# Splitting five of the seven block products of proj once more, for the last two batches of a cross-attention block

## The chip, the core and the metric

The kernel runs on one core of one Trainium2 chip, as one program. The time is device microseconds of that core. TensorE (PE) does the matrix products into PSUM, VectorE (DVE), ScalarE (ACT) and GpSimd (POOL) work on elements, and SyncE (SP) issues most DMAs. [...] Each engine takes its instructions strictly in the order of the program and waits at an instruction until what it needs is there.

## The reference, cut to what matters

```
for each of 4 batches (512 query rows, 512 context rows, D = 512, all float32):
    q, k, v  = layer_norm(x) @ q_w + q_b,  enc @ k_w + k_b,  enc @ v_w + v_b     # 16 heads of 32
    hidden   = softmax(q k^T / sqrt(32), masked) v @ cproj_w + cproj_b + x
    y        = layer_norm(hidden) @ fc_w + fc_b          # 512 x 512 times 512 x 2048
    y        = gelu_tanh(y) @ proj_w + proj_b            # 512 x 2048 times 2048 x 512
    out      = hidden + y
```

The change concerns the last product, proj, of batches two and three (the batches are counted from zero).

## The kernel before, in words

**Stages.** Up to about 550 us the attention of all four batches runs, with the MLP (fc, GELU, proj) of batch zero and half of that of batch one woven into it by lists written out by hand (`first`, `later`). What remains is written out in `last_mlps` (L590): for batch one its second half, then for batches two and three the whole MLP, each as fc, then proj. Within it the order of the program is the order of work on every engine; there is no planner.

**fc.** The 2048 columns of fc are worked off in eight pairs of 128. `fc_seven` (L483) makes a pair as a 2 x 2 block product with seven products in place of eight (Strassen's method in Winograd's form): it needs four sums of the weights and four of the input, and joins the seven products with a few additions. The input's sums are made once per batch by `y_sums` (L472), the sums of the pair's weights by `sum_wa` (L580), one pair ahead. Both run on VectorE. The pair's weights are loaded two pairs ahead by SP into `wa`, their sums lie in `ws`; both are parts of the tile `gt`. TensorE makes the products in the order q1, q26, q57, q34; the second half of q26 (s2 t2) is the first that needs sums. VectorE joins them (L501, L505, L506, L509) into `ga`, and ScalarE applies GELU in place.

**proj.** `project` (L613) does the same for the second product: the activations `ga` are split into four blocks g11, g12, g21, g22, each 128 x 8 chunks x 256, the weights `pb` into b11 to b22. `g_sums` makes the activation sums s1, s2, s4 in `gs` and s3 in place of g21, two chunks at a time under fc. `p_sums` (L584) makes the weight sums t1, t2, t4 in `pt` and t3 in place of b12. Seven products follow: q1, q2, q3, q6, q7, q5, q4. Each is made by `product` (L619) at L622: two row tiles, eight chunks, a matmul with 128 x 128 stationary and 256 moving columns, so 16 matmuls of the program. In float32 the profile records two matmuls for each. VectorE and GpSimd join the products into the residual rows `hid` (`join`, L629); VectorE takes those that lie in PSUM, GpSimd those that were copied to SBUF (`p1p`, `u2p`, `u3p`). SP stores the rows.

**What lies between.** Inside proj the callbacks `sums`, `turns` and `middle` prepare the next batch. `sums` calls `p_sums` and loads the next batch's residual rows (`load_hid`, L397), to which GpSimd adds a bias (`add_row`, L357). `turns` transposes the next batch's normalized rows on TensorE (`ln2_turn`), with two of the four results written by VectorE (L162) and two by ScalarE. `middle` makes `y_sums` of the next batch and `sum_wa(0)`.

**Weights of proj.** Batch one's second half of proj needs only chunk pairs 4 to 7 of `pb`, whose sums are made before `last_mlps`. Pairs 0 to 3 share their place with the attention's keys and queries and with the last batch's rows; they are loaded by SP (L679) under batch two's fc and summed in batch two's `sums`. Batch three uses the same weights and sums again.

**PSUM.** Two pools of four banks each, `ps_acc` and `ps_last`; a block product takes one bank.

## Time and profile before

| | us |
|---|---|
| median of three runs | 803.38 (802.66 to 807.0) |
| the profiled execution, its own time | 801.93 |
| its span, first to last instruction | 800.2 |
| granted TensorE clock, mean | 0.998 |
| TensorE busy | 785.3 (98%) |
| VectorE busy | 573.8 (72%) |
| ScalarE busy | 339.5 (42%) |
| GpSimd busy | 123.9 (15%) |

The stages of `last_mlps` on the span's clock, by where the chain of work passes from one to the next:

| stage | us from the span's start |
|---|---|
| batch one: fc, second half | 552 to 576 |
| batch one: proj, second half | 576 to 601.3 |
| batch two: fc | 601.3 to 649.9 |
| batch two: proj | 649.9 to 700.2 |
| batch three: fc | 700.2 to 748.6 |
| batch three: proj | 748.6 to 800.2 |

The lines of a timeline give the start in us, the time, the engine, the source line, the operation, the tiles out<-in by the program's names, the shapes and how many instructions were merged; in brackets stand the idle time in front and what ended it. The table by stage gives for each engine the busy time in a stretch and the number of instructions, then the granted clock, the busy share of the DMA engines and their GB/s.

### The profile page before, as it was taken

The page shows a single profiled execution, that of the slowest core. Times are in us where ns is not written, and L with a number is a line of the kernel's source. Part 1 is how long each engine was busy: PE and PEld are TensorE (multiplying, and loading weights), DVE is VectorE, ACT ScalarE, POOL GpSimd, SP SyncE. Part 2 cuts the span into 40 slices and gives each one's busy share as a digit, 9 for nine tenths or more (in the row PEclk, how much of TensorE's full clock was granted, in tenths as well). Part 3 has the DMA queues.
Part 4 walks back from the last instruction along what each step waited for, and adds up shares of the span by engine and source line. Part 5 has one row for each costly group of instructions (what it writes and reads, how often), then busy time and mean ns, then how long its engine had stood idle before and what let it go on. Part 6 is the DMA issues. An engine that isn't in the chain of part 4 may idle for free.

```text
span 800.2 us, 12085 instructions
## 1 busy us (share of the span) xinstructions
PE 785.3 (98%) x4178; PEld 499.4 (62%) x4178; DVE 573.8 (72%) x1179; ACT 339.5 (42%) x745; POOL 123.9 (15%) x146
## 2 busy tenths in 40 slices
PE   9999999989999999999999999999999999999998
PEld 6545455456655645556553433446888888888887
DVE  3789998888888857779878988546738983368511
ACT  2567765547763636456554479500201220022100
POOL 1210030055121141001220100020040020200011
PEclk9999999999999999999999999999999999999999
DMA  8889999847897777787777799882325330033001
GB/s 325 289 230 241 235 237 244 231 115 182 209 240 196 211 210 192 179 198 199 181 173 213 205 261 246 202 254 93 117 84 172 118 106 14 27 86 86 1 14 40
DMA packets 60957, 137.15 MB, mean 171 GB/s; under 512 B 12464, under 2 KB 15664, under 8 KB 60768
## 3 DMA queue, kind: packets, MB, share of 16 engines
q1 hardware_dynamic: 59472, 132.43, 61.3%
q0 software_dynamic: 896, 2.82, 1.1%
q10 hardware_dynamic: 528, 1.14, 0.7%
q8 instruction: 33, 0.54, 0.3%
q14 instruction: 28, 0.23, 0.1%
HBM read 58.22 MB, written 6.82 MB: 81 GB/s over the span
## 4 chain that ended last, share of the span: by engine, by line
PE 87%; DVE 6%; SPq 3%; ACT 1%; issue 1%; DMA 1%; POOL 0%; DVEq 0%; POOLq 0%; ACTq 0%
PE q L495 20%; PE accp L554 8%; PE sc L262 7%; PE accc L386 7%; PE av L345 7%; PE accv L240 6%; PE acck L218 6%; PE accq L228 5%; PE accf L536 3%; DVE ptt L266 3%; SPq L328 2%; PE q4p L622 2%; PE q3p L622 2%; PE q5p L622 2%; PE q6p L622 2%; PE q7p L622 2%
## 5 line engine op out<-in xcount | busy, mean ns | idle before, releaser
L270 ACT ACTIVATE ptt<-ptt,mn 128x512 f32<-128x512 f32 x256 | 181.7, 711 | 135.1 <-DVE mn L266 134.8
L266 DVE CUSTOM_DVE_ANT_0 ptt<-sc,mb 128x512 f32<-128x512 f32 x256 | 161.0, 685 | 32.7 <-PE sc L262 32.4
L285 DVE STREAM_TRANSPOSE tb<-ptt 128x1024 f32<-128x1024 f32 x96 | 119.2, 1242 | 14.4 <-ACT ptt L270 12.9
L554 PE MATMUL accp<-pbt,gt 128*128 128x512 f32 x192 | 86.7, 600 | 0.0
L495 PE MATMUL q<-yT,gt 128*128 128x256 f32 x320 | 78.9, 379 | 0.0
L262 PE MATMUL sc<-pbt 32*128 32x512 f32 x512 | 73.0, 640 | 4.7 <-DVE mn L266 2.5
L513 ACT ACTIVATE ga<-ga,vec 128x512 f32<-128x512 f32 x40 | 26.7, 714 | 93.2 <-DVE ga L455 93.2
L495 PEld LDWEIGHTS q<-yT,gt 128*128 128x128 f32 x320 | 60.8, 190 | 8.7 <-issue 0.5
L554 PEld LDWEIGHTS accp<-pbt,gt 128*128 128x128 f32 x192 | 35.2, 190 | 49.0 <-issue 46.4
L240 PEld LDWEIGHTS accv<-ptt,xe 128*128 128x128 f32 x512 | 58.7, 192 | 9.5 <-issue 6.7
L495 PE MATMUL q<-ys,gt 128*128 128x256 f32 x240 | 61.8, 380 | 0.5 <-DVE ys L452 0.5
L240 PE MATMUL accv<-ptt,xe 128*128 128x128 f32 x512 | 60.8, 277 | 0.0
L218 PE MATMUL acck<-xe,ptt 128*128 128x512 f32 x128 | 59.1, 605 | 0.0
L228 PE MATMUL accq<-xe,ptt 128*128 128x512 f32 x128 | 58.4, 599 | 0.0
L386 PE MATMUL accc<-wc,oT 128*128 128x512 f32 x128 | 56.6, 596 | 0.0
L495 PEld LDWEIGHTS q<-ys,gt 128*128 128x128 f32 x240 | 45.4, 190 | 7.4 <-DVE ys L452 0.9
L345 PE MATMUL av<-pT,v 128*32 128x256 f32 x768 | 48.1, 392 | 1.8 <-DMA gt<-tb 0.7
L498 ACT COPY p<-q 128x256 f32<-128x256 f32 x28 | 9.9, 355 | 92.5 <-PE q L495 92.5
L270 ACT ACTIVATION_READ_ACCUMULATOR ptt<-ptt,mn 128x1 f32 x256 | 47.8, 187 | 0.0
L252 POOL TENSOR_TENSOR v<-v,row 128x512 f32<-128x512 f32 x16 | 20.4, 1275 | 172.9 <-ACT v L245 172.8
L228 PEld LDWEIGHTS accq<-xe,ptt 128*128 128x128 f32 x128 | 23.6, 190 | 32.4 <-issue 30.4
L262 PEld LDWEIGHTS sc<-pbt 32*128 32x128 f32 x512 | 20.0, 182 | 37.9 <-issue 21.4
(137 smaller groups left out, 1071.4 us busy)
## 6 DMA issues: line engine op xcount, KB each, us to landing
pT<-tb SPq DMA_DIRECT2D x384, 136.0 KB, 2.4
pbt<-p_w_dram SPq DMA_DIRECT2D x40, 256.0 KB, 3.1
gt<-fc_w_dram SPq DMA_DIRECT2D x40, 256.0 KB, 2.6
gt<-tb SPq DMA_DIRECT2D x64, 136.0 KB, 3.4
xe<-tb SPq DMA_DIRECT2D x56, 136.0 KB, 3.1
pbt<-fc_w_dram SPq DMA_DIRECT2D x24, 256.0 KB, 3.9
ptt<-k_w_dram SPq DMA_DIRECT2D x16, 256.0 KB, 3.8
xe<-encT_dram SPq DMA_DIRECT2D x16, 256.0 KB, 4.6
```

The costliest lines, as they stand in the source:

```text
L218: nc.tensor.matmul(acc, S["wk", w][:, d, :], eT[:, d, :], start=(d == 0), stop=(d == ND - 1))
L228: nc.tensor.matmul(acc, S["wq", w][:, d, :], xT[:, d, :], start=(d == 0), stop=(d == ND - 1))
L240: nc.tensor.matmul(acc[:, ts(t, P)], eT[:, d, ts(t, P)], S["wv", w][:, d, :], start=(d == 0), stop=(d == ND - 1),)
L262: nc.tensor.matmul(sc[:, h, :], qT[r, ts(qt, P)], kT[r, :], start=True, stop=True)
L266: nc.vector.tensor_tensor_reduce(out=s, in0=sc[:, h, :], in1=S["mb", w // NG], scale=1.0, scalar=FMAX, op0=ALU.add, op1=ALU.min, accum_out=mn,
L270: nc.scalar.activation(s, s, AF.Exp, bias=mn, scale=-1.0, accum_out=sums[:, qt, h : h + 1])
L285: nc.vector.transpose(*two_heads[k])
L345: nc.tensor.matmul(av[ts(h, HD), : 2 * P].rearrange(shape, **kw), v[:, t, ts(h, HD)], p[t][h], start=(t == 0), stop=(t == NT - 1),)
L386: nc.tensor.matmul(acc, S["oT", b][:, g, ts(t, P)], wc[:, g, :], start=(g == 0), stop=(g == NG - 1))
L495: nc.tensor.matmul(o, x[:, k], y[:, k], start=(k == 0), stop=(k == 1))
L554: nc.tensor.matmul(acc, gT[q % 2][:, k, ts(t, P)], S["pw", b, q * FQ + k], start=(k == 0), stop=(k == FQ - 1))
L622: nc.tensor.matmul(o[:, t], a[:, c, ts(t, P)], w[:, c], start=(c == pairs[0]), stop=(c == pairs[-1]))
```

## The change

Only `last_mlps` is touched.

- For batches two and three, five of the seven products of proj (q2, q3, q6, q7, q5) are each made by the same method once more: a new function `forty_nine` splits the block of 8 chunks x 256 rows and the block of 8 chunks x 256 columns in four quarters each and makes seven products of four chunks, with 128 stationary and 128 moving columns. A product of 16 matmuls becomes seven of four, so 28 matmuls with half as many moving columns. q1 and q4 stay whole.
- `x_sums` makes the activation sums of a product: three on VectorE (one in place), one on GpSimd. The three that need room go where a block has been used up (`free`), or for q2 into unused parts of `gt`.
- `w_sums` makes the weight sums of a product. Batches two and three share them, in the new tile `tt` and in `wsum`. Those of q2 and q3 are made in batch one's proj in front of q5, two operations on VectorE and two on GpSimd each; those of q6, q7 and q5 are called in fc pairs 0, 1 and 2 of batch two, all four operations on GpSimd.
- The seven small products are joined by VectorE, four additions, into `u2p`, `u3p` or `p1p`, and from there into `hid`: q2's and q3's by GpSimd, q5's by VectorE. ScalarE copies the first small product of each.
- For that, the weights of chunk pairs 0 to 3 are loaded under batch one's fc, no longer under batch two's, and their `p_sums` are made in batch one's proj.
- Each of the five products takes two tiles of each PSUM pool.

```diff
+        p1s = last.tile([P, 2, P], F32, tag="p1s", name="p1s")
+        tt = last.tile([P, 4, 3, NP // 2, P], F32, tag="tt", name="tt")
...
+        def quarters(m):
+            return [m[:, i * NP // 2 : (i + 1) * NP // 2, ts(j, P)] for i in range(2) for j in range(2)]
+
+        def w_sums(i, w, engine=None):
+            w11, w12, w21, w22 = quarters(w)
+            t1, t2, t4 = more(i)
+            sub(t1, w12, w11, engine)
+            sub(t2, w22, t1, engine)
+            sub(w12, w22, w12, nc.gpsimd)
+            sub(t4, w21, t2, nc.gpsimd)
+
+        def x_sums(x, free):
+            x11, x21, x12, x22 = quarters(x)
+            s1, s2, s4 = free if isinstance(free, list) else quarters(free)[:3]
+            add(nc.vector, s1, x21, x22)
+            sub(s2, s1, x11)
+            sub(x21, x11, x21)
+            sub(s4, x12, s2, nc.gpsimd)
+
+        def forty_nine(b, name, o, x, w, free, i):
...
+            def product(r, x, w):
+                for c in range(NP // 2):
+                    nc.tensor.matmul(r, x[:, c], w[:, c], start=(c == 0), stop=(c == NP // 2 - 1))
+
+            product(r1[:, 0], x11, w11)
+            nc.scalar.copy(p1, r1[:, 0])
+            product(r26[:, 0], x12, w21)
+            product(r26[:, 1], s2, t2)
+            add(nc.vector, o[:, 0:4:3], r26[:, :2], p1[:, None, :].broadcast_to([P, 2, P]))
+            product(r57[:, 1], s3, t3)
+            product(r57[:, 0], s1, t1)
+            add(nc.vector, o[:, 1:3], r57[:, :2], o[:, 3:4].broadcast_to([P, 2, P]))
+            add(nc.vector, o[:, 3], r57[:, 0], o[:, 2])
+            product(r34[:, 0], s4, w22)
+            product(r34[:, 1], x22, t4)
+            add(nc.vector, o[:, 1:3], r34[:, :2], o[:, 1:3])
...
+            if b > SPLIT:
+                x_sums(g12, x_more)
+                x_sums(s4, g11)
+                forty_nine(b, "2", u3p, g12, b21, x_more, 4)
+                turns()
+                join(nc.gpsimd, 0, 0, p1p)
+                join(nc.gpsimd, 0, 0, u3p)
+                store(0, 0)
+                x_sums(s2, g12)
+                forty_nine(b, "3", u3p, s4, b22, g11, 0)
+                join(nc.gpsimd, 0, 1, u3p)
+                x_sums(s3, s4)
+                forty_nine(b, "6", u2p, s2, t2, g12, 1)
+                add(nc.vector, u2p, u2p, p1p)
+                x_sums(s1, s2)
+                forty_nine(b, "7", u3p, s3, t3, s4, 2)
+                add(nc.vector, u3p, u3p, u2p)
+                for i, j, src in ((0, 1, u2p), (1, 0, u3p), (1, 1, u3p)):
+                    join(nc.gpsimd, i, j, src)
+                forty_nine(b, "5", p1p, s1, t1, s2, 3)
+                join(nc.vector, 0, 1, p1p)
+                join(nc.vector, 1, 1, p1p)
+            else:
...
+                w_sums(4, b21)
+                w_sums(0, b22)
                 q5 = half_tile(f"q5p_{b}")
...
-            (SPLIT, range(half, NP), ()), (SPLIT + 1, range(NP), range(half)), (SPLIT + 2, range(NP), ())
+            (SPLIT, range(half, NP), range(half)), (SPLIT + 1, range(NP), ()), (SPLIT + 2, range(NP), ())
...
-                if c in new:
-                    for i in range(2):
-                        nc.sync.dma_start(out=pb[:, c, i, :], in_=p_w[ts(2 * c + i, P), :])
+                if b == SPLIT + 1 and c < 3:
+                    w_sums(c + 1, (pt[:, 1], pb[:, :, 0, HL:], pt[:, 0])[c], nc.gpsimd)
                 fc_pair(b, c, lambda: sum_wa(c + 1) if c + 1 < NP else None)
...
+                if c - half in new:
+                    for i in range(2):
+                        nc.sync.dma_start(out=pb[:, c - half, i, :], in_=p_w[ts(2 * (c - half) + i, P), :])
```

More of the change, by code (lines that the diff above doesn't have):

```diff
@@ L598, in last_mlps, with more @@
         p1p, u2p, u3p = (last.tile([P, 2, HL], F32, tag=n, name=n) for n in ("p1p", "u2p", "u3p"))
+        p1s = last.tile([P, 2, P], F32, tag="p1s", name="p1s")
+        tt = last.tile([P, 4, 3, NP // 2, P], F32, tag="tt", name="tt")
+        w_more = wsum.rearrange("p a s k f -> p (a s k) f")
+        x_more = [
+            gt[:, n : n + NP // 2 * P].rearrange("p (c n) -> p c n", c=NP // 2) for n in (1024, 1536, 3072)
+        ]
+        def more(i):
+            return [w_more[:, 4 * n : 4 * n + 4] if i == 4 else tt[:, i, n] for n in range(3)]
@@ new lines, in forty_nine @@
+        def forty_nine(b, name, o, x, w, free, i):
+            x11, s3, x12, x22 = quarters(x)
+            s1, s2, s4 = free if isinstance(free, list) else quarters(free)[:3]
+            w11, t3, w21, w22 = quarters(w)
+            t1, t2, t4 = more(i)
+            r1, r26 = (acc_tile(f"{n}{name}_{b}").rearrange("p (i n) -> p i n", i=4) for n in ("r1", "r26"))
+            r57, r34 = (
+                ps_last.tile([P, 4, P], F32, tag="half", name=f"{n}{name}_{b}") for n in ("r57", "r34")
+            )
+            o = o.rearrange("p t (j n) -> p (t j) n", j=2)
+            p1 = p1s[:, i % 2]
+            def product(r, x, w):
[13 more added lines that the diff above has]
+            add(nc.vector, o[:, 1:3], r34[:, :2], o[:, 1:3])
@@ L635, in store @@
                     nc.sync.dma_start(out=out[b, ts(2 * i + t, P), j * HL : (j + 1) * HL], in_=hid(i, j, t))
-            q1, q2 = (acc_half(f"{n}p_{b}") for n in ("q1", "q2"))
+            q1 = acc_half(f"q1p_{b}")
             product(q1, g11, b11)
@@ L640, in project @@
             sums()
-            product(q2, g12, b21)
-            turns()
-            q3 = half_tile(f"q3p_{b}")
-            product(q3, s4, b22)
-            join(nc.vector, 0, 0, q2)
-            join(nc.gpsimd, 0, 0, p1p)
-            store(0, 0)
-            q6 = acc_half(f"q6p_{b}")
-            product(q6, s2, t2)
-            add(nc.vector, u2p, q6, p1p)
-            join(nc.vector, 0, 1, q3)
-            q7 = half_tile(f"q7p_{b}")
-            product(q7, s3, t3)
-            add(nc.vector, u3p, q7, u2p)
@@ L655, in project @@
-            for i, j, src in ((0, 1, u2p), (1, 0, u3p), (1, 1, u3p)):
-                join(nc.gpsimd, i, j, src)
-            q5 = half_tile(f"q5p_{b}")
-            product(q5, s1, t1)
-            join(nc.vector, 0, 1, q5)
-            join(nc.vector, 1, 1, q5)
+            if b > SPLIT:
[21 more added lines that the diff above has]
+            else:
+                q2 = acc_half(f"q2p_{b}")
+                product(q2, g12, b21)
+                turns()
+                q3 = half_tile(f"q3p_{b}")
+                product(q3, s4, b22)
+                join(nc.vector, 0, 0, q2)
+                join(nc.gpsimd, 0, 0, p1p)
+                store(0, 0)
+                q6 = acc_half(f"q6p_{b}")
+                product(q6, s2, t2)
+                add(nc.vector, u2p, q6, p1p)
+                join(nc.vector, 0, 1, q3)
+                q7 = half_tile(f"q7p_{b}")
+                product(q7, s3, t3)
+                add(nc.vector, u3p, q7, u2p)
+                for i, j, src in ((0, 1, u2p), (1, 0, u3p), (1, 1, u3p)):
+                    join(nc.gpsimd, i, j, src)
+                w_sums(4, b21)
+                w_sums(0, b22)
+                q5 = half_tile(f"q5p_{b}")
+                product(q5, s1, t1)
+                join(nc.vector, 0, 1, q5)
+                join(nc.vector, 1, 1, q5)
```

## The prediction

> **What bounds the kernel now.** I read the page, the chain that ended last, the table by stage, then the timeline at the two places where the change puts GpSimd beside VectorE.

> ```profile
> PE 785.3 (98%) x4178; PEld 499.4 (62%) x4178; DVE 573.8 (72%) x1179; ACT 339.5 (42%) x745; POOL 123.9 (15%) x146
> ```

> TensorE works 98% of the span, so only fewer TensorE cycles, or a new hole in them, move the time. The chain in order of time (start, us, engine, tile, line, matmuls; each fp32 matmul of the program leaves two):

> ```profile
> 253.45 3.57 PE accv L240 x32
> ...
> 601.32 1.73 PE q L495 x8
> 603.05 46.89 PE q L495 x216
> 649.94 6.91 PE q1p L622 x32
> 656.85 6.91 PE q2p L622 x32
> ```

> A block product of batches two and three is 32 matmuls of 256 columns: 6.91/32 = 0.216 us each. `accv` has the form that the change uses, 128 columns with a weight load for each: 3.57/32 = 0.112 us.

> ```profile
> core 0: us, PE busy (x) PEld busy (x) DVE busy (x) ACT busy (x) POOL busy (x), PEclk, DMA share, GB/s
> ...
> 173.50:176.80 3.30, 3.30 (x32) 1.32 (x27) 2.24 (x4) 0.66 (x1) 1.61 (x1) 0.50 0.00 0
> ...
> 601.30:649.90 48.60, 48.59 (x226) 42.46 (x225) 43.91 (x90) 11.50 (x22) 1.37 (x2) 1.00 0.41 130
> 649.90:700.20 50.30, 50.30 (x242) 44.23 (x241) 22.85 (x35) 3.48 (x5) 11.48 (x12) 1.00 0.13 43
> ```

> In batch two's fc (601.3 on) VectorE is busy 43.9 of 48.6 us; in its proj (649.9 on) only 22.9 of 50.3. The first row is the one stretch at half clock: TensorE had stood still from 169.6 to 172.7. The start of batch two's fc, timeline:

> ```profile
> 599.31 0.68 DVE L452 TENSOR_TENSOR ys<-yT 128x512 f32<-128x512 f32 x1
> ...
> 601.31 0.68 DVE L452 TENSOR_TENSOR ys<-yT,ys 128x512 f32<-128x512 f32 x1
> 601.91 0.42 DVE L455 TENSOR_TENSOR gt<-gt 128x256 f32<-128x256 f32 x1
> 602.24 1.21 DVE L452 TENSOR_TENSOR gt<-gt 128x256 f32<-128x256 f32 x3
> ...
> 603.05 0.73 PEld L495 LDWEIGHTS q<-ys,gt 128*128 128x128 f32 x4 [0.41 <-DVE gt L452]
> ```

> Here there is no slack: four `y_sums` (599.31 to 601.99) and the first three of `sum_wa(0)` end at 603.0, where TensorE's third product (s2 t2) waits for them. What GpSimd does to such VectorE operations, batch two's proj:

> ```profile
> 653.35 1.27 POOL L357 TENSOR_TENSOR hid<-hid,row 128x512 f32<-128x512 f32 x1 [23.58 <-DMA hid<-xa]
> 653.41 1.76 DVE L452 TENSOR_TENSOR gs<-gs,ga 128x512 f32<-128x512 f32 x1
> 655.08 4.62 POOL L357 TENSOR_TENSOR hid<-hid,row 128x512 f32<-128x512 f32 x3 [0.47 <-DMA hid<-xa]
> 655.20 1.70 DVE L452 TENSOR_TENSOR gs<-ga,gs 128x512 f32<-128x512 f32 x1
> 656.83 1.76 DVE L452 TENSOR_TENSOR ptt<-pbt 128x512 f32<-128x512 f32 x1
> 658.62 1.64 DVE L452 TENSOR_TENSOR ptt<-pbt,ptt 128x512 f32<-128x512 f32 x1
> 660.18 0.68 DVE L452 TENSOR_TENSOR pbt<-pbt 128x512 f32<-128x512 f32 x1
> ```

> While GpSimd adds, each VectorE operation with both inputs in SBUF starts 1.69 us after the one before (653.41 to 660.18 over four) instead of 0.62: the engines take turns. Operations that read PSUM do not suffer (L162 at 583.0: 0.81 us beside GpSimd).

> **The change part by part.** Products: seven of 8 matmuls = 56 x 0.1116 = 6.25 us, against 6.91. Ten of them (five a batch): -6.6 us. Bounds by the slowest `accv` chain (3.77) and the shortest pitch (0.109): 6.60 and 6.10, so -3.1 to -8.1; I take the common row.

> [...]

> Sums and joins in proj: a product costs VectorE three sums (0.62 apart) and four joins (0.42 for 256 elements, less for 128), 3.4 us, and GpSimd one sum of 1.27. Even with two sums held up (+2.1) that is 5.5 of 6.25 us, made one product ahead: nothing, uncovered it would be 2 a product. One place lacks cover. In batch two VectorE reaches the sums of g12 at 656.83, and its first two meet GpSimd's last `hid` adds and end at 660.26, where `ptt` ended above; TensorE, two small products in, wants them at 656.85 + 1.79 = 658.64. Cost 1.6. If GELU ends 3.9 after fc's end and not 2.1 (the walk below), four `g_sums` meet all four adds (6.8) and two sums follow (1.3): 12.0, against 0.9 + 6.9 + 1.8 = 9.6: cost 2.4. Batch three loads no `hid`: sums done 6.1 after fc's end, wanted at 8.7: nothing. The last product's joins, `y_sums` and `sum_wa(0)` take 5.7 us under q4's 6.91 plus 1.7 of fc: nothing.

> Moved: `p_sums` of the first four pairs go from batch two's proj to batch one's, where products take 3.45. VectorE, free at 580.4, has eight operations, three beside GpSimd's remaining `hl` adds: 3 x 1.69 + 5 x 0.63 = 8.2, to 588.6; two turns 1.5, two joins 0.7: 590.8. Its next work waits for q6p until 590.96, and q3p, q6p wait for ScalarE's turns and for `gs` (580.5): nothing, by 0.2 us. Their eight weight loads go into batch one's fc. SP issues them at 557 at the earliest, behind the `xa` stores of 550.9; behind them the `hl` loads slip 0.85 us, which moves the same collisions: nothing. Five copies of 128 columns a batch on ScalarE, busy 3.5 of 50: nothing.

> New: `w_sums`. The diff places twelve GpSimd sums in fc pairs 0 to 2 of batch two, but in the built program they carry no wait on fc: GpSimd runs them as soon as it is through with batch one. The walk, on the trace's clock:
> - 595.1: u3p is done. VectorE makes four weight sums while GpSimd makes its four joins of 0.72: four turns of about 1.1, to 599.3. Then the joins of q5, from PSUM, 1.4: 600.6, against 599.31 before.
> - GpSimd is free at 599.95 and holds 16 sums of 1.27 back to back, 20 us alone.
> - VectorE: four `y_sums` and three of `sum_wa(0)`, taking turns. The first finds a GpSimd sum half done (1.1), then 3 x 1.69 and 3 x 1.42 (256 wide, 0.27 shorter): 10.4, to 611.0.
> - TensorE stands from 603.05 to 611.0: 8.0 us (7.3 to 8.8 by the shortest and longest turns shown, 1.56 and 1.79). Behind that wait in its queue lies all of fc; behind VectorE's, the joins of q4, and behind those SP's stores and the next `wa` load, which fc pair 2 needs 9 us later.
> - The clock: 3.05 us of standstill cost 3.4 us at half speed, 1.7; after 8 us as much, bounds 0 and 3.4.
> - GpSimd ends near 623, having also held up `sum_wa(1)` (four turns, 4.3) and part of `sum_wa(2)` (1.5). At 613.1 VectorE has fc still before it: 10 of `sum_wa`, 20 of joins, 8 of `g_sums`, 5 of statistics and norms, with those turns 49: to 662.1, GELU 1.4 later. TensorE ends fc at 649.94 + 8.0 + 1.7 = 659.6 and q1p wants the last pair 3.0 later, 662.6: 0.9 us, bounds 0.4 and 1.5.

> Sum: -6.6 + 8.0 + 1.7 + 0.9 + 2.4 = +6.4. Against the profiled execution (800.2 span, 801.93 in all): 808.3. The median of the three runs lies 1.45 above that execution: 803.38 + 6.4 = 809.8, say 810. With all bounds one way (-8.1 + 7.3 + 0 + 0.4 + 1.6; -3.1 + 8.8 + 3.4 + 1.5 + 2.4) 804.6 and 816.4; its likely range is 805 to 814.

> [...]

> **Rivals.**
> - GpSimd lets VectorE through (its paired sums wait for one another, and VectorE could take two turns in that gap). Then the sums take 3.7 from 600.6, as from 599.31 before: a stall of 1.2, and -6.6 + 1.2 + 1.6 = -3.8: 799.6, not slower. For it: the 0.08 us gap behind dependent GpSimd sums. Against: four turns in strict alternation above. It decides if at most two of the seven are held up (1.2 + 2 x 1.07 + 1.6, and 1.7 of clock, = 6.6).
> - VectorE becomes the bound of batch two's fc: it has 4.7 us to spare, and if each of the 16 weight sums costs it a turn (16 x 1.07 = 17) some 5 more reach TensorE: 809.8 + 5 = 815. Against: its joins read PSUM, which lets GpSimd pass.
> - The small products gain nothing (weight loads of 0.19 us come in a row of 56): 809.8 + 6.6 = 816.4. Against: `accv`, 16 in a row.

> **How the numbers follow.** As walked 0.60; GpSimd yields 0.20; VectorE bound 0.12; no gain 0.08. A measurement here can tell about 0.5%, 4 us: faster is below 799.4, slower above 807.4. The first case is slower with 0.52 and same with 0.08; the second lies on the limit, 0.10 each; the others are slower: 0.10, 0.18, 0.72. Range: from inside the yielding case, 801, to 816.

> **What would show it.** Right: seven small products in 6.25 us; TensorE idle some 8 us in front of batch two's first s2 t2, released by VectorE's `gt` sums; `y_sums` of about 1.7 us there beside 1.7 us GpSimd sums; clock 0.5 just after; 1 to 3 us of wait in front of batch two's r26. Wrong: `y_sums` near 0.7 beside GpSimd, or GpSimd starting its sums well after 600.

## The result, and the profile after

| | before | changed |
|---|---|---|
| median of 8 runs, us | 803.29 (801.65 to 807.0) | 809.92 (808.12 to 811.47) |
| profiled execution, us | 801.93 | 808.12 |
| span, us | 800.2 | 805.9 |

The changed kernel is slower: ratio 1.0079, 95% interval 1.0058 to 1.0101. The page of the changed kernel, busy time by engine:

```profile
PE 779.3 (97%) x4418; PEld 502.3 (62%) x4418; DVE 629.1 (78%) x1245; ACT 342.1 (42%) x755; POOL 173.2 (21%) x180
```

TensorE has 6.0 us less to do than before (785.3) and yet ends 5.7 us later. What stopped it, from 570 us on (waits of TensorE: who waits for whom, us in total, times, longest):

```profile
PE q L495 <- DVE gt L452: 7.7, 1, 7.7
PE r L643 <- DVE gt L452: 2.4, 1, 2.4
PE q1p L680 <- ACT ga L513: 0.2, 1, 0.2
```

The last of the three stands in the trace of before too, as the only one there:

```profile
PE q1p L622 <- ACT ga L513: 0.2, 1, 0.2
```

The other two are new. The first is in front of batch two's fc; the timelines of TensorE, VectorE and GpSimd there:

```profile
610.44 2.07 PE L495 MATMUL q<-ys,gt 128*128 128x256 f32 x4 [7.73 <-DVE gt L452]
```

```profile
600.05 1.11 DVE L452 TENSOR_TENSOR ys<-yT 128x512 f32<-128x512 f32 x1
601.27 1.57 DVE L452 TENSOR_TENSOR ys<-yT,ys 128x512 f32<-128x512 f32 x1
602.77 1.74 DVE L452 TENSOR_TENSOR yT<-yT 128x512 f32<-128x512 f32 x1
604.44 1.75 DVE L452 TENSOR_TENSOR ys<-yT,ys 128x512 f32<-128x512 f32 x1
```

```profile
599.35 1.27 POOL L452 TENSOR_TENSOR pbt<-pbt 128x512 f32<-128x512 f32 x1
600.58 1.72 POOL L452 TENSOR_TENSOR wsum<-pbt,wsum 128x512 f32<-128x512 f32 x1
602.26 1.71 POOL L452 TENSOR_TENSOR pbt<-pbt 128x512 f32<-128x512 f32 x1
...
621.10 1.45 POOL L452 TENSOR_TENSOR tt<-ptt,tt 128x512 f32<-128x512 f32 x1
```

The starts alternate between the engines: 600.58 GpSimd, 601.27 VectorE, 602.26, 602.77. The last two `y_sums` shown start 1.67 us apart, where before each took 0.68. GpSimd runs its 16 weight sums with no pause above 0.1 us from 599.35 to 622.55, although twelve of them are written under fc pairs 0 to 2.

The table by stage for the standstill and what follows (busy us and instructions of PE, PEld, DVE, ACT, POOL; then the granted clock):

```profile
605.15:610.44 5.29, 0.00 (x0) 0.00 (x0) 5.26 (x5) 0.00 (x0) 5.21 (x5) 0.50 0.00 0
610.44:615.39 4.95, 4.95 (x12) 3.96 (x13) 4.95 (x6) 0.00 (x0) 4.87 (x4) 0.50 0.33 106
```

Half clock begins in the standstill and lasts 4.95 us into the work. Last, the gain, in the chain that ended last (start, us, engine, tile, line, matmuls):

```profile
764.50 31.26 PE r L643 x280
```

Five products in 31.26 us are 6.25 each, against 6.91.

The part ahead of the last two batches differs from execution to execution (in the traces shown here batch one's last product ends between 600.3 and 607.1 us), so the stages are compared by length, each from the end of one TensorE product to the end of another. The experiments stand in the same table. Each row is one execution, the profiled one; times are good to 0.01 us.

| us | batch two: fc | proj | batch three: fc | proj | sum | against before |
|---|---|---|---|---|---|---|
| before | 48.62 | 50.31 | 48.35 | 48.34 | 195.62 | |
| changed | 58.77 | 49.49 | 48.35 | 45.07 | 201.68 | +6.06 |
| e1, no weight sums | 48.62 | 48.62 | 48.35 | 45.08 | 190.67 | -4.95 |
| e2, none of the twelve | 55.34 | 48.36 | 48.35 | 45.08 | 197.13 | +1.51 |
| e3, the twelve on VectorE | 56.13 | 50.14 | 48.35 | 45.08 | 199.70 | +4.08 |
| e4, sums behind the joins | 49.70 | 50.21 | 48.34 | 45.08 | 193.33 | -2.29 |
| e5, `hid` adds spread | 58.70 | 46.83 | 48.34 | 45.08 | 198.95 | +3.33 |
| e6, both | 48.62 | 47.78 | 48.35 | 45.08 | 189.83 | -5.79 |
| e7, fewer in the last pair | 48.62 | 47.54 | 48.35 | 45.08 | 189.59 | -6.03 |

The profiled executions of the changed kernel and of e4 are the fastest of theirs (808.12 and 799.02 us), those of e1, e3 and e7 the slowest, so stages and medians do not differ by the same amounts; the medians of before and changed lie 6.63 apart.

### The profile page after: what moved, and what is told of

The parts are those of the page before. It is cut to its first block, busy times and chain, and to the rows that moved or that the text cites. A ratio compares the mean times of both kernels' runs of the same rounds, so it can differ in the third digit from the quotient of the medians.

```text
span 805.9 us, 12735 instructions
## 1 busy us (share of the span) xinstructions
PE 779.3 (97%) x4418; PEld 502.3 (62%) x4418; DVE 629.1 (78%) x1245; ACT 342.1 (42%) x755; POOL 173.2 (21%) x180
## 4 chain that ended last, share of the span: by engine, by line
PE 80%; DVE 12%; SPq 4%; issue 2%; ACT 1%; DMA 1%; POOL 0%; DVEq 0%; POOLq 0%; ACTq 0%
PE q L495 16%; PE accp L554 8%; PE r L643 8%; PE sc L262 7%; PE accc L386 7%; PE accv L240 7%; PE av L345 7%; PE acck L218 6%; PE accq L228 5%; SPq L328 4%; PE accf L536 3%; DVE ptt L266 2%; DVE ga L455 2%; PE q4p L680 2%; PE tp L159 1%
## 5 line engine op out<-in xcount | busy, mean ns | idle before, releaser
L495 PE MATMUL q<-yT,gt 128*128 128x256 f32 x320 | 79.7, 382 | 0.0
L495 PE MATMUL q<-ys,gt 128*128 128x256 f32 x240 | 63.4, 388 | 8.2 <-DVE gt L452 7.7
L495 PEld LDWEIGHTS q<-yT,gt 128*128 128x128 f32 x320 | 61.4, 192 | 9.0 <-issue 0.5
L240 PEld LDWEIGHTS accv<-ptt,xe 128*128 128x128 f32 x512 | 58.6, 192 | 9.7 <-issue 6.3
L240 PE MATMUL accv<-ptt,xe 128*128 128x128 f32 x512 | 60.9, 277 | 0.0
L495 PEld LDWEIGHTS q<-ys,gt 128*128 128x128 f32 x240 | 46.5, 195 | 15.5 <-DVE gt L452 8.1
L345 PE MATMUL av<-pT,v 128*32 128x256 f32 x768 | 46.4, 382 | 2.9 <-DMA gt<-tb 0.8
L386 PEld LDWEIGHTS accc<-wc,oT 128*128 128x128 f32 x128 | 23.8, 190 | 31.5 <-issue 29.8
```

What stands on the lines that cost most here:

```text
L240: nc.tensor.matmul(acc[:, ts(t, P)], eT[:, d, ts(t, P)], S["wv", w][:, d, :], start=(d == 0), stop=(d == ND - 1),)
L345: nc.tensor.matmul(av[ts(h, HD), : 2 * P].rearrange(shape, **kw), v[:, t, ts(h, HD)], p[t][h], start=(t == 0), stop=(t == NT - 1),)
L386: nc.tensor.matmul(acc, S["oT", b][:, g, ts(t, P)], wc[:, g, :], start=(g == 0), stop=(g == NG - 1))
L495: nc.tensor.matmul(o, x[:, k], y[:, k], start=(k == 0), stop=(k == 1))
```

## The experiments

The theory: the small products gain what the arithmetic says, and GpSimd's new sums take it back because they run beside VectorE operations with both inputs in SBUF, at a place where TensorE waits for those. The rivals: VectorE's own extra work, or GpSimd's weight sums wherever they lie. All edits are against the changed kernel.

**e1: no weight sums at all.**

```diff
-                w_sums(4, b21)
-                w_sums(0, b22)
...
-                if b == SPLIT + 1 and c < 3:
-                    w_sums(c + 1, (pt[:, 1], pb[:, :, 0, HL:], pt[:, 0])[c], nc.gpsimd)
```

> The changed kernel with all twenty new weight sums left out (the small products read old numbers for them), so the split, the activation sums and the joins stand alone. Theory (the split gains 6.6 us, and GpSimd's weight sums, which hold up VectorE, take it back): no wait in front of batch two's fc, y_sums at 0.69 us, the small products at 6.25 a block product, a wait of 1.6 us in batch two's second product from the hid adds. -6.6 + 1.6 = -5.0 against before: about 798.3 us. Rival (VectorE is overloaded by activation sums and joins, whatever GpSimd does): waits between the products of proj stay, 803 or more.

Measured: 797.85 us (before 803.03, ratio 0.9913, 0.9882 to 0.9945). The small products then read numbers that no sum has written. The wait in front of fc is gone and fc takes 48.62 us, as before the change. What is left of TensorE's waits, beside the 0.2 us at q1p:

```profile
PE r L642 <- DVE gt L452: 0.7, 1, 0.7
PE r L642 <- DVE ga L452: 0.6, 1, 0.6
```

These 1.3 us (1.6 expected) lie in batch two's second product and belong to the `hid` adds. So the small products gain, and the weight sums, GpSimd's and VectorE's together, cost all of what was lost in fc.

**e2: the twelve sums called under fc left out.** The eight of batch one's proj stay; three of the five products read numbers that no sum of theirs has written.

```diff
-                if b == SPLIT + 1 and c < 3:
-                    w_sums(c + 1, (pt[:, 1], pb[:, :, 0, HL:], pt[:, 0])[c], nc.gpsimd)
```

> The changed kernel with the twelve weight sums that are called under fc left out (three of the five products then read old numbers); the eight of batch one's proj stay, four of them on GpSimd. Theory (each VectorE sum that meets a GpSimd sum loses 1 us): the four y_sums are held up as in the changed kernel, sum_wa(0) is not. TensorE waits 4.5 us in front of the first s2 t2 instead of 7.7, then some 2 us for the clock and 1.6 to 2.4 in batch two's proj: -6.6 + 4.5 + 2 + 1.8 = +1.7, about 805 us. Rival (VectorE comes late because of its own four weight sums, and the twelve do nothing): as the changed kernel, 810.

Measured: 804.15 us, ratio 1.0011 (0.9993 to 1.003): no difference that can be told. TensorE's wait there, timeline:

```profile
607.57 2.08 PE L495 MATMUL q<-ys,gt 128*128 128x256 f32 x4 [4.53 <-DVE gt L452]
```

The four GpSimd sums of batch one's proj are enough for a standstill of 4.53 us, since they too run while VectorE makes `y_sums`. Not all of it comes from that meeting: `y_sums` begins only 0.94 us ahead of fc's first product, where it was 2.01 before the change, because VectorE has weight sums of its own to make first; e4 shows this part, about 1.1 us, by itself. With half clock behind the standstill, the stage loses 6.72 us, which eats the gain.

**e3: the twelve on VectorE, in the same place.**

```diff
-            sub(w12, w22, w12, nc.gpsimd)
-            sub(t4, w21, t2, nc.gpsimd)
+            sub(w12, w22, w12, engine or nc.gpsimd)
+            sub(t4, w21, t2, engine or nc.gpsimd)
...
-                    w_sums(c + 1, (pt[:, 1], pb[:, :, 0, HL:], pt[:, 0])[c], nc.gpsimd)
+                    w_sums(c + 1, (pt[:, 1], pb[:, :, 0, HL:], pt[:, 0])[c], nc.vector)
```

> The changed kernel with the twelve weight sums of fc on VectorE, at the same place in the program, four in each of fc pairs 0 to 2. Theory (the shared access to SBUF costs, not the work): VectorE gets 12 x 0.62 = 7.4 us of work and loses some 11 us of waiting. TensorE waits 4.5 us in front of the first s2 t2 as GpSimd still holds four sums, 2 for the clock, 1.5 at q1p for VectorE's backlog, 2.6 in batch two's second product: -6.6 + 10.6 = +4.0, about 807 us. Rival (any further work for VectorE at this place reaches TensorE in full): 810 or more.

Measured: 807.62 us, ratio 1.0052 (1.003 to 1.0075). TensorE's waits, and VectorE's share of the rest of fc by the table by stage:

```profile
PE q L495 <- DVE gt L452: 5.5, 3, 4.5
PE r L643 <- DVE gt L452: 2.2, 1, 2.2
PE q1p L680 <- ACT ga L513: 0.8, 2, 0.6
```

```profile
614.29:663.19 48.90, 47.89 (x216) 41.24 (x215) 46.51 (x92) 11.14 (x21) 1.37 (x2) 0.98 0.28 87
```

The stop in front of fc is the 4.53 us of e2, so it comes from the four sums that stayed on GpSimd. With twelve more operations VectorE is busy 46.5 of 48.9 us, and waits of 0.55, 0.46 and 0.55 us appear inside and behind fc. By the stages the twelve cost 4.55 us on GpSimd (+6.06 against e2's +1.51) and 2.57 on VectorE (+4.08). The second figure would be some 0.8 larger if the stop of 4.53 us had been followed by as much half clock as in e2 (4.49 us of work at half speed there, 2.86 in e3). So at this place they cost on either engine; e4 asks whether another time is better.

**e4: the same 16 GpSimd sums, two in each fc pair, started by VectorE's first join.** A tiny GpSimd operation reads what that join has written, and so holds the sums until VectorE has turned to operations that read PSUM.

```diff
             add(nc.vector, g[:, 0:4:3], q26, p1[:, None, :].broadcast_to([P, 2, HL]))
+            joined()
...
+        def two_sums(c):
+            nc.gpsimd.tensor_scalar(gate, ga[:, c, 0, 0:4], 1.0, 0.0, ALU.mult, ALU.add)
+            for _ in range(2):
+                sub(*later_sums.pop(0), nc.gpsimd)
```

> The changed kernel with the same sixteen GpSimd sums, two in each of batch two's eight fc pairs, held back by a tiny GpSimd operation that reads what VectorE's first join of that pair wrote; they then run beside the joins, which read PSUM. Theory: y_sums and sum_wa(0) run at 0.69 and 0.42 us, TensorE waits 1.0 us there since VectorE is 0.75 late from its own weight sums, no half clock; under fc each pair costs VectorE at most 0.8 us, of which some 0.5 in all reach TensorE; 2 us in batch two's second product: -6.6 + 1.0 + 0.5 + 2.0 = -3.1, about 800 us. Rival (GpSimd sums cost VectorE a turn each wherever they stand): 16 x 1.07 = 17, less 4.7 to spare, 808 or more.

Measured: 802.14 us, ratio 0.998 (0.9959 to 1.0002): no difference that can be told. By the stages it is -2.29 us, where -3.1 and 800 us were expected. In the trace no half clock follows fc's beginning. That trace has one interval of half clock in all, 3.41 us long (172.37 us on), and a granted clock of 0.998; the other nine executions have 0.996 (eight) or 0.994, which by an estimate is one or two such intervals more (3.41 us at half speed take 0.002 off the mean of 797 us), and where those lie no trace shows. TensorE's waits:

```profile
PE r L654 <- DVE gt L452: 2.3, 1, 2.3
PE q L495 <- DVE gt L452: 1.1, 1, 1.1
PE q1p L691 <- ACT ga L514: 0.8, 2, 0.6
```

Of 7.7 us of standstill 1.1 is left, with every sum still made on GpSimd. That 1.1 is no longer a collision at `y_sums` (four in a row, 0.6 to 0.8 us apart): VectorE comes to them later, because its own weight sums in front of q5's joins meet GpSimd's joins (three of the four take 1.10 to 1.21 us instead of 0.69), and `y_sums` begins 0.92 us ahead of fc where it was 2.01 before the change. VectorE's timeline:

```profile
594.02 0.68 DVE L452 TENSOR_TENSOR wsum<-pbt 128x512 f32<-128x512 f32 x1
594.74 1.10 DVE L452 TENSOR_TENSOR wsum<-pbt,wsum 128x512 f32<-128x512 f32 x1
595.76 1.21 DVE L452 TENSOR_TENSOR tt<-pbt 128x512 f32<-128x512 f32 x1
597.01 1.10 DVE L452 TENSOR_TENSOR tt<-pbt,tt 128x512 f32<-128x512 f32 x1
...
599.36 0.68 DVE L452 TENSOR_TENSOR ys<-yT 128x512 f32<-128x512 f32 x1
```

**e5: the `hid` adds spread over batch two's proj.** Each goes where GpSimd has just joined a block.

```diff
-        for t in ts_:
-            add_row(S["hid", b, t], 1)
+        if b < B - 1:
+            for t in ts_:
+                add_row(S["hid", b, t], 1)
...
+        def hid_row(b, t):
+            if b + 1 < B:
+                add_row(S["hid", b + 1, t], 1)
...
                 store(0, 0)
+                hid_row(b, 0)
                 x_sums(s2, g12)
                 forty_nine(b, "3", u3p, s4, b22, g11, 0)
                 join(nc.gpsimd, 0, 1, u3p)
+                hid_row(b, 1)
```

The other two follow behind q6's addition and q7's joins.

> The changed kernel with one thing moved: the four GpSimd adds of the bias to batch three's residual rows, which met VectorE in front of batch two's second product, are put one behind each of q2's, q3's, q6's and q7's small products. Theory: the wait of 2.4 us there goes, and each add costs VectorE one turn where it has over 2 us to spare; 2.4 less than the changed kernel, about 807.5 us. Rival (the sums of g12 come too late because VectorE is behind from fc): at most 0.8 less, 809 or more.

Measured: 808.12 us (before 803.52), ratio 1.0059 (1.0037 to 1.0082), and 2.73 us less than the changed kernel by the stages. The stop of 7.7 us stays, the one of 2.4 us is gone, and proj falls from 49.49 to 46.83 us. TensorE's waits, beside the 0.2 us at q1p:

```profile
PE q L496 <- DVE gt L453: 7.7, 1, 7.7
```

So without the `hid` adds in that place there is no second wait. How long it is with them depends on when VectorE gets there: 1.3 us in e1, 2.4 in the changed kernel.

**e6: e4 and e5 together,** and the two VectorE weight sums of q2 moved up to the place behind q3's join, where VectorE would wait for q7.

```diff
                 join(nc.vector, 0, 1, q3)
+                w_sums(4, b21)
                 q7 = half_tile(f"q7p_{b}")
...
-                w_sums(4, b21)
                 w_sums(0, b22)
```

> The last run's order (sixteen GpSimd weight sums two by two behind VectorE's first join of each fc pair) with the residual adds spread as in the run beside it, and VectorE's two weight sums of b21 made while it waits for q7 instead of in front of the joins of q5. Theory: the wait in front of the first s2 t2 goes (1.1 to 0.1), 0.6 at q1p stays, the 2.3 us in batch two's second product go: -6.6 + 0.1 + 0.6 = -5.9 against before, about 797.3 us, and no weight sum is left out. Rival (GpSimd's work costs the same wherever it stands): 800 or more, as when only the sixteen were moved.

Measured: 797.92 us (795.47 to 798.35), ratio to before 0.9922 (0.9902 to 0.9941). It makes every sum that the change makes, and is faster than both kernels. Timelines of GpSimd and VectorE in fc's first pair, then TensorE's only wait:

```profile
607.84 0.20 POOL L628 TENSOR_SCALAR gate<-ga 128x4 f32<-128x4 f32 x1 [7.41 <-DVE ga L456]
608.00 1.27 POOL L453 TENSOR_TENSOR pbt<-pbt 128x512 f32<-128x512 f32 x1
609.23 1.28 POOL L453 TENSOR_TENSOR wsum<-pbt,wsum 128x512 f32<-128x512 f32 x1
```

```profile
607.85 1.15 DVE L456 TENSOR_TENSOR ga<-q,ga 128x512 f32<-128x512 f32 x2
609.23 0.69 DVE L456 TENSOR_TENSOR ga<-q,ga 128x512 f32<-128x512 f32 x1 [0.23 <-PE q L496]
```

```profile
PE q1p L696 <- ACT ga L515: 0.9, 2, 0.7
```

GpSimd's sums take 1.27 and 1.28 us, VectorE's joins 0.58 (two in 1.15) and 0.69: beside each other, neither engine is held up. The two sums of q2 still take 1.10 us each, beside GpSimd's joins, but where VectorE has the time: `y_sums` begins 2.01 us ahead of fc again (600.87), and fc is back at 48.62 us. The shortest stages of all runs (e5's proj of 46.83 us, the other three as here) would give -6.74; -5.79 remains. The 0.95 us between them go with the wait in q1p, behind the last pair (0.7 us of idle TensorE).

Not every GpSimd sum keeps to the joins, though. In the last two pairs the second one runs on into the VectorE operations behind them, a `g_sums` of 0.68 us alone and a normalization of 0.54 alone (VectorE, then GpSimd):

```profile
648.11 1.52 DVE L456 TENSOR_TENSOR gs<-ga 128x512 f32<-128x512 f32 x1
...
654.25 1.06 DVE L150 TENSOR_SCALAR hn<-hn,mv,rs 128x512 f32<-128x512 f32 x1
```

```profile
647.81 1.28 POOL L453 TENSOR_TENSOR tt<-ptt,tt 128x512 f32<-128x512 f32 x1
...
653.76 1.28 POOL L453 TENSOR_TENSOR tt<-ptt,tt 128x512 f32<-128x512 f32 x1
```

VectorE ends fc's last joins 2.84 us behind TensorE's last product of fc, where it was 0.73 before the change.

**e7: e6 with one sum in the last fc pair and three in the second.**

```diff
-            for _ in range(2):
+            for _ in range({1: 3, 7: 1}.get(c, 2)):
```

> As the run beside it, with one of the sixteen weight sums moved from fc pair 7 to pair 1, where VectorE has statistics between its joins and the next sums. Theory: the 0.6 us at q1p come from VectorE's last normalization, held up by the second sum of pair 7; without it -6.4 against before, about 796.8 us. Rival (VectorE is behind anyway at the end of fc): as the run beside it.

Measured: 798.74 us (796.8 to 800.11), ratio 0.9942 (0.9925 to 0.996), where 796.8 was expected. The wait at q1p falls by 0.24 us (0.69 to 0.45), and the stages by as much; the times of the two overlap and cannot tell such a step. The cause that was expected is not it: VectorE's last normalization takes 0.54 us again (it was 1.06 in e6), but in both kernels it starts behind the last joins, and the wait is still there. What the traces show is that VectorE ends those joins late, 2.60 us behind TensorE (2.84 in e6). Which of the delays before that make the lateness stays open.

## Why the prediction was right, step by step

Forecast 810.0 us, measured 809.92; +6.4 us in the sum of terms, +6.06 in the stages. Term by term:

- **The gain.** Predicted -6.6 us for ten products. Batch three's proj fell from 48.34 to 45.07 us, -3.27. Batch two's takes 46.83 us in e5, where its new wait is gone, -3.48; of that 0.21 are the turns (1.96 to 1.75 us in the chain), which the sum did not have, and 3.27 the products. So the ten products gained 6.54. The row of 128-column matmuls at 0.112 us each carried over exactly, and with it falls the rival in which the small products gain nothing.
- **The stall.** Predicted 8.0 us from 603.05, measured 7.73 from 602.71. The walk was right in kind: GpSimd did start at once, and all seven VectorE sums were held up, so the rival in which GpSimd yields is out as well. Of the 7.73 us some 1.1 are VectorE's late arrival, as e4 shows; the walk had that, 600.6 against 599.31. VectorE came to `y_sums` at 600.05 (600.6 predicted) and the third sum of `sum_wa(0)` ended at 610.39 (611.0). Turns were 1.67 us for 512 columns (1.69 predicted) and 1.40 to 1.48 for 256 (1.42).
- **The clock.** Predicted 1.7 us, with bounds 0 and 3.4. Measured: 4.95 us of work at half speed, so 2.5 lost; the stage shows 58.77 - 48.62 - 7.73 = 2.42. The term was too small by 0.7, because one half-clock interval of 3.4 us was carried over from the standstill of before, which was 3.05 us long.
- **q1p's wait for the last pair.** Predicted 0.9 us, measured none beyond the 0.2 of before. Here the walk failed: VectorE took up `sum_wa(1)` at 612.39 and not at 613.1, and ended its last joins at 661.2 and not at 662.1, just in time. The rival in which VectorE bounds fc asked for some 5 us more than the forecast and is out with it; e3, with twelve more operations on VectorE, shows where that bound begins.
- **Batch two's second product.** Predicted 2.4 us, measured 2.40 of idle TensorE; against e5, which has no such wait, it cost 2.66. The size is nearly right, but the absolute times were not: the sums ended 11.0 us after fc's end (12.0 predicted), and TensorE wanted them at 8.7 (9.6), both some 0.9 earlier for want of the wait at q1p. The first of the four `g_sums` escaped, which the walk did not have, and q2's first sum was caught instead, so that the size owes something to luck, as the timelines of VectorE and GpSimd show:

```profile
662.61 0.69 DVE L455 TENSOR_TENSOR gs<-ga 128x512 f32<-128x512 f32 x1 [0.95 <-ACT ga L513]
...
668.33 1.74 DVE L455 TENSOR_TENSOR gt<-ga 128x512 f32<-128x512 f32 x1
```

```profile
664.84 4.68 POOL L357 TENSOR_TENSOR hid<-hid,row 128x512 f32<-128x512 f32 x3 [0.34 <-DMA hid<-xa]
```

- **What was put at nothing.** `p_sums` in batch one's proj did not stop TensorE. VectorE was through with q2's joins at 590.57 (590.8 predicted), 0.05 us before q6 ended at 590.62. The earlier weight loads stopped nothing either: from the end of batch one's fc to the end of its proj every kernel takes 26.65 us, and its fc 22.73 in the chain of before and of changed. Nor did ScalarE's copies: the five products of batch three run without a wait, 31.26 us in a row.

The misses of the sum nearly cancel: +0.7 in the clock and +0.3 at the second product against -0.9 at q1p, -0.3 in the stall and -0.2 in the turns. That the total is better than its terms is luck, and so is 810.0 against 809.92.

## What to carry to other kernels

That GpSimd is idle does not make work on it free: in this kernel what decides is which VectorE operations it runs beside (`y_sums` of 0.68 us came 1.67 us apart, joins from PSUM still took 0.69), and what slack those have. Sums that are needed only much later can be tied to the moment at which VectorE turns to operations on PSUM, by one tiny instruction that reads a result of VectorE; in this kernel that turned +6.06 us into -5.79, together with the `hid` adds spread over proj and two VectorE sums moved to where VectorE had time for them. Before giving GpSimd work, look in the program built for the wait that it really carries: here its place in the source held nothing back.

## What the runs showed of the hardware

**Turns.** A GpSimd sum of 1.27 us alone and a VectorE sum of 0.68 alone run at one pair per some 1.68 us where they meet (1.67 at `y_sums`, 1.58 to 1.78 at the `hid` adds, both in the changed kernel), less than the 1.95 that the two add up to. These VectorE sums have both inputs in SBUF. e6's joins, with one input in PSUM, are not held (0.69 us beside GpSimd's 1.28). The normalization at L150, with one large SBUF input, is (1.06 us beside a GpSimd sum in e6, 0.54 alone in e7).
